# Depthwise taps of one channel block on TensorE in the first two chunks, and stores on other queues

## The chip, the cores and the metric

The kernel runs on one core of a Trainium2 chip. A core has four engines that compute, each with its own list of instructions that it works off in order: TensorE (PE: matrix products into the accumulators, PSUM), VectorE (DVE), ScalarE (ACT) and GpSimd (POOL). A fifth, SyncE (SP), only issues transfers. ACT and POOL issue transfers too. The engines wait for each other by semaphores. The metric is device time in microseconds (us), the median over runs; less is better.

## The reference, cut to what matters

Two layers work on an image batch of 2 x 512 channels x 64 x 64 pixels. The first is a deformable convolution, the second an attention with normalization; the change touches the first alone.

```python
inp = jnp.transpose(x, (0, 2, 3, 1))                 # x is the group-normalized input
xproj = inp @ in_w + in_b
x1 = conv(x, dw_w, 3x3, one filter per channel)      # depthwise
x1 = jnp.transpose(x1, (0, 2, 3, 1)) + dw_b
mu = x1.mean(-1, keepdims=True)
var = ((x1 - mu) ** 2).mean(-1, keepdims=True)
x1 = (x1 - mu) / jnp.sqrt(var + LN_EPS) * ln_g + ln_b
x1 = jax.nn.gelu(x1, approximate=False)
offset = x1 @ off_w + off_b
mask = jax.nn.softmax((x1 @ mask_w + mask_b).reshape(N, H, W, G, P), -1)
out = _dcnv3_core(xproj, offset, mask)               # 9 sampled points per pixel and group
out = out @ out_w + out_b
...
x = x + out
```

The depthwise convolution is nine taps per channel: each output pixel is the sum of nine neighbours, each times a weight of its channel.

## The kernel before, in words

Everything is float32. The 512 channels are four blocks (KB) of 128 partitions; an image is 8 chunks of 512 pixels (8 rows), so the two images are 16 chunks. The first layer is a pipeline over chunks with these stages, each a Python generator whose `yield`s cut it into steps:

- `project(i)` (p0, p1, p2 for the first chunks): ScalarE writes the normalized rows of a chunk with a border row on each side into `xn` (L762, four blocks), then in four tiles TensorE multiplies `xn` with `in_w` into `pq` (L772), ScalarE copies `pq` to `xj` (L778), and two stores write `xj` to the padded image `xt` in memory (L780). There is one `xn`: the next chunk's rows are written over it block by block.
- `features(i)` (f0, f1, f): for each block ScalarE computes the tap in the middle of the upper row with the bias (L798), then VectorE adds the other eight taps, one instruction each (L806). For chunks 0 and 1 (`fill`) TensorE forms the mean over all channels with a matrix of ones (L822, `p_mean`) from the four blocks of `conv`; VectorE subtracts it (L827); ScalarE squares (L832, into `feat`, or `awT` for chunk 1); TensorE forms the mean of the squares (L822 again); ScalarE takes the root (L840, `rstd`), VectorE the reciprocal (L842) and multiplies (L843); ScalarE applies the Gelu (L849, `feat`).
- `weights(i)` (v, w): TensorE multiplies `feat` with the offset and mask weights in four tiles (L866, `po`), VectorE adds the bias (L871); then the exponential (L878), the distances `tx` (L883, L884), a Relu (L890), the softmax sums (L893 to L898), `my` (L901) and 17 instructions that build the window weights `aw` (L909, L914); ScalarE copies them to `at` (L919) and TensorE transposes them (L928).
- `sample(i)` (y, m): TensorE spreads the weights (L957, `pb`), ScalarE or VectorE copies them to `bt` (L962), TensorE multiplies them with patches of `xt` (L976, `pa`; the patches are loaded by `fetch`, L941), then comes the output projection (L996).

Beside them run `image_stats(1)` (`more`: statistics of the second image, VectorE L727, loads from POOL's queue L714), `value_weights` (`products`: a product for the second layer, L1129, with a ScalarE copy `wc_part` L1133 and a store to `wvfc` L1134), and `border()`, 16 stores that write the frame of `xt` (L698, L699).

The pipeline stands in a hand-written order: within `tc.manual_schedule()` the program calls `p0()`, `f0(8)` and so on, and each engine's list is exactly the order in which these calls reach its instructions. The part before the first full `period` is the fill: chunk 0 and 1 have nothing else to run beside. Accumulators with the tag `mm` have four buffers, shared by `pq`, `p_mean`, `pw`, `po` and others in the order of their use. `xj` and `wc_part` share two buffers. `next_to_last` is the order for the last chunk but one: y is the sampling of the chunk before, m that of its own, w the weights of the last chunk.

Of the kernel before, what the change touches and what calls it, by code (L numbers as in the profile page):

```python
# [10 lines left out]
F32 = mybir.dt.float32  # L11
I32 = mybir.dt.int32
AF = mybir.ActivationFunctionType
# [5 lines left out]
P = 128  # L19
NB = 2  # L20
C = 512
KB = C // P
H = W = 64
# [6 lines left out]
NP = 9  # L30
GP = G * NP
CH = 512
NCH = S // CH
ROWS = CH // W
# [484 lines left out]
WIN = W + 4  # L519
# [35 lines left out]
def window_path(  # L555
# [3 lines left out]
    nc = tc.nc  # L559
# [8 lines left out]
    wc_d = dram.tile([P, KB, C], F32, name="wvfc")  # L568
# [13 lines left out]
    ident = const.tile([P, P], F32, name="ident")  # L582
# [43 lines left out]
    with ExitStack() as l0:  # L626
# [68 lines left out]
        def border():  # L695
            for n in range(NB):
                for e in (0, 1, WIN - 2, WIN - 1):
                    nc.sync.dma_start(xt_d[n][e], edge[:WIN, :])  # L698
                    nc.sync.dma_start(xt_d[n][2 : H + 2, e, :], edge[:H, :])  # L699

        gn = {}

# [35 lines left out]
        def project(i):  # L738

            n, ch = divmod(i, NCH)  # L740
            sc, bi = gn[n]
            lo, hi = max(ch * ROWS - 1, 0), min(ch * ROWS + ROWS + 1, H)
            r0 = lo - (ch * ROWS - 1)
            raws = deque()

            def read(kb):
                if i < 3:
                    raws.append(img[kb][:, lo * W : hi * W].rearrange("p (r c) -> p r c", c=W))
                else:
                    t = io.tile([P, ROWS + 2, W], F32, name="raw", bufs=3)  # L750
                    nc.sync.dma_start(t[:, : hi - lo, :].rearrange("p r c -> p (r c)"), x_v[n, :, kb, lo * W : hi * W])
                    raws.append(t[:, : hi - lo, :])

            for kb in range(3):
                read(kb)
            yield
            if ch == 0:
                nc.gpsimd.memset(xn[:, :, 0, :], 0.0)
            if ch == NCH - 1:
                nc.gpsimd.memset(xn[:, :, ROWS + 1, :], 0.0)  # L760
            for kb in range(KB):
                nc.scalar.activation(  # L762
                    xn[:, kb, r0 : r0 + hi - lo, :], raws.popleft(),
                    AF.Identity, bias=bi[:, kb : kb + 1], scale=sc[:, kb : kb + 1],
                )
                if kb + 3 < KB:
                    read(kb + 3)
                yield
            for t in range(ROWS // 2):
                pq = ps.tile([P, C], F32, tag="mm", name="pq")  # L770
                for kb in range(KB):
                    nc.tensor.matmul(  # L772
                        pq, xn[:, kb, 1 + 2 * t : 3 + 2 * t, :].rearrange("p r c -> p (r c)"), in_w[:, kb, :],
                        start=(kb == 0), stop=(kb == KB - 1),
                    )
                yield
                xj = io.tile([P, C], F32, name="xj", bufs=2)
                nc.scalar.copy(xj, pq)  # L778
                for r in range(2):
                    nc.sync.dma_start(xt_d[n][2 + ch * ROWS + 2 * t + r, 2 : W + 2, :], xj[r * W : (r + 1) * W, :])  # L780
                yield

        feats = {}
        conv = cv.tile([P, KB, CH], F32, name="conv")

        def features(i):

            a = cv.tile([P, KB, CH], F32, tag="dT", name="conv1", bufs=2) if i == 1 else conv
            def tap_of(kb, tap):
                dy, dx = tap // 3, tap % 3 - 1  # L790
                acc = a[:, kb, :].rearrange("p (r c) -> p r c", c=W)
                src = xn[:, kb, dy : dy + ROWS, max(dx, 0) : W + min(dx, 0)]
                return acc[:, :, max(-dx, 0) : W + min(-dx, 0)], src, dw_w[:, kb, tap : tap + 1]


            for kb in range(KB):
                dst, src, wt = tap_of(kb, 1)
                nc.scalar.activation(dst, src, AF.Identity, bias=dw_b[:, kb : kb + 1], scale=wt)  # L798
                if i != 2 or kb == KB - 1:
                    yield  # L800
            fill = i < 2
            tot = None if fill else sm.tile([P, CH], F32, tag="tot", name="tot")
            for kb in range(KB):
                for tap in (0, 2, 3, 4, 5, 6, 7, 8):
                    dst, src, wt = tap_of(kb, tap)
                    nc.vector.scalar_tensor_tensor(dst, src, wt, dst, ALU.mult, ALU.add)  # L806
                    if tap < 8:
                        yield

                if not fill:  # L810
                    if kb == 0:
                        nc.gpsimd.dma_start(tot, a[:, 0, :])
                    elif kb < KB - 1:
                        nc.gpsimd.dma_start(tot, a[:, kb, :], accum_op=ALU.add)
                    else:
                        nc.vector.tensor_add(tot, tot, a[:, kb, :])
                yield

            def mean_over_c(tot):
                p = ps.tile([P, CH], F32, tag="mm", name="p_mean")  # L820
                for k, x in enumerate(tot):
                    nc.tensor.matmul(p, ones, x, start=(k == 0), stop=(k + 1 == len(tot)))  # L822
                return p

            mu = mean_over_c([a[:, kb, :] for kb in range(KB)] if fill else [tot])
            yield
            nc.vector.tensor_sub(a, a, mu.unsqueeze(1).to_broadcast([P, KB, CH]))  # L827
            f = awT.rearrange("p g w -> p (g w)").rearrange("p (k c) -> p k c", k=KB)
            if i != 1:
                f = cv.tile([P, KB, CH], F32, tag="feat", name="feat")  # L830
            for kb in range(KB):
                nc.scalar.activation(f[:, kb, :], a[:, kb, :], AF.Square)  # L832
            yield
            if not fill:
                nc.vector.tensor_add(f[:, 0:2, :], f[:, 0:2, :], f[:, 2:4, :])
                nc.vector.tensor_add(f[:, 0, :], f[:, 0, :], f[:, 1, :])
                yield
            var = mean_over_c([f[:, kb, :] for kb in range(KB if fill else 1)])
            rstd = sm.tile([P, CH], F32, tag="tot", name="rstd")
            nc.scalar.activation(rstd, var, AF.Sqrt, bias=eps)  # L840
            yield
            nc.vector.reciprocal(rstd, rstd)  # L842
            nc.vector.tensor_mul(a, a, rstd.unsqueeze(1).to_broadcast([P, KB, CH]))  # L843
            if i == 1:
                f = cv.tile([P, KB, CH], F32, tag="feat", name="feat")
            yield

            for kb in range(KB):
                nc.scalar.activation(  # L849
                    f[:, kb, :].rearrange("p (c q) -> p c q", c=PC), a[:, kb, :].rearrange("p (q c) -> p c q", c=PC),  # L850
                    AF.Gelu, bias=ln_b[:, kb : kb + 1], scale=ln_g[:, kb : kb + 1],
                )
                if kb % 2:
                    feats[i] = f
                    yield
# [231 lines left out]
        def next_to_last(y, v, m, w):  # L1087

            y(3)
            w(8)  # L1090
            v(4)
            for steps, tiles in ((1, 2), (1, 2), (2, 1), (1, 0)):
                m(2)
                w(steps)
                y(tiles)
            for _ in range(4):
                m(2)
                w(2)
            w(5)
# [24 lines left out]
        def value_weights():  # L1124

            for cb in range(KB):
                pw = ps.tile([P, C], F32, tag="mm", name="pw")
                for kb in range(KB):
                    nc.tensor.matmul(  # L1129
                        pw, wv[:, kb, cb * P : (cb + 1) * P], wf[kb], start=(kb == 0), stop=(kb == KB - 1)  # L1130
                    )
                t = io.tile([P, C], F32, tag="xj", name="wc_part", bufs=2)
                nc.scalar.copy(t, pw)  # L1133
                nc.sync.dma_start(wc_d[:, cb, :], t)  # L1134
                yield

        def output_bias():
# [16 lines left out]
        with tc.manual_schedule():  # L1154
# [3 lines left out]
            p0()  # L1158
            for kb in range(KB):
                p0()  # L1160
                f0()
            for t in range(4):
                p0(2)
                f0(8)
            border()
            more()
            p1()
            for kb in range(KB):
                p1()
                f1()  # L1170
                if kb == 1:
                    next(products)
                    next(products)
            f0()
            f1(5)
            p1(4)
            f0()
            f1(11)
            f0()
# [1 line left out]
                more()  # L1181
            p1(4)
            f0(3)
            f1(16)
            next(products)
            fetch(0, 0)
            fetch(0, 1)
# [845 lines left out]
```

## Time and profile before

| what | us |
|---|---|
| median of 3 runs | 3322.8 (3321.55 to 3323.41) |
| the profiled execution | 3318.6 |
| its span in the profile | 3316.8 |
| PE busy | 3148.9 (95%) |
| DVE busy | 2731.0 (82%) |
| ACT busy | 1342.3 (40%) |
| fill: start of the first tap (DVE) to its end of `aw` for chunk 0 | 38.5 to 140.3 |
| first layer, to the last residual addition of the output projection | 1158.3 |

Busy times are from the engine list of the page; the fill's ends are VectorE rows of the timeline. In a timeline a row is a run of like instructions: start in the span, duration, engine, line, operation, output<-input, shape, count, and in brackets the idle time before it with what ended it. An engine's row without a bracket followed the one before directly. In the page's forty slices each digit is the busy share of a slice of some 83 us in tenths, so the fill is the first two slices.

### The profile page before, as it was taken

To read this page: it belongs to the slowest core of one execution; us is meant where nothing else is said; L and a number is where in the kernel's file an instruction comes from. 1 tells how busy PE (TensorE), PEld (TensorE's weight loads), DVE (VectorE), ACT (ScalarE), POOL (GpSimd) and SP (SyncE) were. 2 spreads that over 40 slices of the span, in tenths; PEclk is the share of its full clock that TensorE was granted. 3 is DMA by queue.
4 is the path that set the end of the run, shared out by engine and by line. 5 is a ranking of instruction groups with operands and counts; after the bars stand their busy time and mean duration, and the time that the engine had idled before them with its cause. 6 is when DMAs were issued, how large, how long until landed. Compare 5 with 4: busy or idle time off the path is not lost. (4 is left out here: it accounts for less than half of the span.)

```text
span 3316.8 us, 38421 instructions
## 1 busy us (share of the span) xinstructions
PE 3148.9 (95%) x14207; PEld 2263.5 (68%) x14207; DVE 2731.0 (82%) x3907; ACT 1342.3 (40%) x1848; POOL 291.7 (9%) x420
## 2 busy tenths in 40 slices
PE   5899999999999899999999999999999999999993
PEld 2455555555555676787877877887687787787782
DVE  7999999999998689885976967968897796886874
ACT  2678888888886533203113122123211202203114
POOL 1100000000000000001000011000001101001022
PEclk9999999999999999999999999999999999999996
DMA  7435543443444278658667677557667758648689
GB/s 240 123 117 155 158 117 115 139 147 108 125 136 136 95 284 260 195 171 224 197 174 216 190 218 201 188 195 243 221 202 203 203 180 237 193 163 237 195 311 375
DMA packets 241237, 629.07 MB, mean 190 GB/s; under 512 B 28528, under 2 KB 45552, under 8 KB 240016
## 3 DMA queue, kind: packets, MB, share of 16 engines
q1 hardware_dynamic: 177952, 413.37, 37.5%
q0 software_dynamic: 51936, 179.86, 20.5%
q10 hardware_dynamic: 11152, 33.30, 2.7%
q8 instruction: 114, 1.87, 0.2%
q14 instruction: 83, 0.68, 0.1%
HBM read 406.61 MB, written 124.91 MB: 160 GB/s over the span
## 5 line engine op out<-in xcount | busy, mean ns | idle before, releaser
L1566 PE MATMUL accy<-tt,v 128*128 128x256 f32 x1944 | 580.2, 380 | 0.7 <-DVE ct L1632 0.6
L1456 ACT ACTIVATE e<-pS 128x1024 f32<-128x1024 f32 x256 | 248.3, 1021 | 736.1 <-PE pS L1451 731.9
L1566 PE MATMUL accx<-e,v 128*128 128x256 f32 x1728 | 453.5, 385 | 0.5 <-DMA v<-wv 0.5
L1566 PE MATMUL accy<-e,v 128*128 128x256 f32 x1728 | 445.2, 380 | 0.0
L1566 PEld LDWEIGHTS accy<-tt,v 128*128 128x128 f32 x1944 | 369.6, 190 | 53.8 <-DVE tt L1524 2.2
L1566 PEld LDWEIGHTS accx<-e,v 128*128 128x128 f32 x1728 | 320.5, 190 | 118.3 <-issue 77.9
L806 DVE SCALAR_TENSOR_TENSOR conv<-xn,L_conv_dw_w_sb,conv 128x504 f32<-128x504 f32 (+1 forms) x512 | 376.8, 744 | 29.2 <-ACT conv L798 15.3
L1566 PEld LDWEIGHTS accy<-e,v 128*128 128x128 f32 x1728 | 329.5, 191 | 45.2
L1524 DVE TENSOR_TENSOR tt<-tt,e 128x512 f32<-128x512 f32 x432 | 298.9, 692 | 14.8
L1566 PE MATMUL accx<-tt,v 128*128 128x256 f32 x972 | 290.7, 381 | 14.0 <-DVE tt L1523 14.0
L1523 DVE TENSOR_TENSOR tt<-e 128x256 f32<-128x256 f32 x432 | 181.0, 419 | 141.1 <-PE accy L1566 138.8
L976 PEld LDWEIGHTS pa<-bt,patch 96*128 96x128 f32 x2048 | 248.4, 195 | 57.1 <-issue 38.8
L976 PE MATMUL pa<-bt,patch 96*128 96x128 f32 x2048 | 252.4, 280 | 7.6 <-issue 4.0
L1451 PE MATMUL pS<-q,keys 64*128 64x512 f32 x1024 | 254.7, 615 | 0.3 <-DVE stats L1789 0.3
L962 ACT COPY bt<-pb 96x1024 f32<-96x1024 f32 x120 | 226.2, 2024 | 45.8 <-PE pb L957 45.8
L772 PE MATMUL pq<-in_w,xn 128*128 128x512 f32 x512 | 234.6, 601 | 3.4 <-ACT xn L762 3.4
L996 PE MATMUL py<-dT,L_conv_out_w_sb 128*128 128x512 f32 x512 | 230.0, 593 | 0.0
L1571 ACT COPY u<-accx 128x256 f32<-128x256 f32 x54 | 20.1, 372 | 477.0 <-PE accx L1566 474.2
L1566 PEld LDWEIGHTS accx<-tt,v 128*128 128x128 f32 x972 | 184.6, 190 | 41.0 <-DVE tt L1523 16.0
L987 ACT COPY dT<-pa 32x256 f32<-32x256 f32 x496 | 179.5, 362 | 62.3 <-PE pa L976 53.4
L866 PE MATMUL po<-om_w_pg,feat 128*128 128x432 f32 x512 | 203.6, 542 | 0.8 <-ACT feat L849 0.8
L996 PEld LDWEIGHTS py<-dT,L_conv_out_w_sb 128*128 128x128 f32 x512 | 95.5, 190 | 114.3 <-issue 107.4
(292 smaller groups left out, 4381.5 us busy)
## 6 DMA issues: line engine op xcount, KB each, us to landing
v<-wv SPq DMA_DIRECT2D x420, 448.0 KB
tot<-e POOLq DMA_DIRECT2D x160, 512.0 KB, 6.8
patch<-xt SPq DMA_DIRECT2D x256, 192.0 KB
wv<-vform SPq DMA_DIRECT2D x48, 512.0 KB
v<-ww SPq DMA_DIRECT2D x54, 448.0 KB
wv<-vsum SPq DMA_DIRECT2D x48, 384.0 KB
xt<-xj SPq DMA_DIRECT2D x128, 128.0 KB
res<-in_x SPq DMA_DIRECT2D x64, 256.0 KB
```

The lines of the kernel that those rows point to most:

```text
L772: nc.tensor.matmul(pq, xn[:, kb, 1 + 2 * t : 3 + 2 * t, :].rearrange("p r c -> p (r c)"), in_w[:, kb, :], start=(kb == 0), stop=(kb == KB ...
L806: nc.vector.scalar_tensor_tensor(dst, src, wt, dst, ALU.mult, ALU.add)
L866: nc.tensor.matmul(po[:, : 3 * GP], f[:, kb, t * P : (t + 1) * P], om_w[:, kb].rearrange("p a k g -> p (a k g)"), start=(kb == 0), stop=(k ...
L962: copy(bt[:SN].rearrange("s g q d -> s d (g q)")[:, d0 : d0 + 4, :], pb[:SN])
L976: nc.tensor.matmul(pa[:, p], xp[:SN, p, cb * P : (cb + 1) * P], bt[:SN, 4 * cb : 4 * cb + 4, PX * s + p, :], start=True, stop=True,)
L987: copy(dst, src)
L996: nc.tensor.matmul(py, out_w[:, kb, cb * P : (cb + 1) * P], dT[:, kb, :], start=(kb == 0), stop=(kb == KB - 1))
L1451: nc.tensor.matmul(p[:, a, :], keys[r, i, (2 * u + h) * P : (2 * u + h + 1) * P], c.q[r, qh, :], start=True, stop=True,)
L1456: nc.scalar.activation(e.rearrange("p a q -> p (a q)"), p.rearrange("p a q -> p (a q)"), AF.Exp)
L1523: nc.vector.tensor_sub(t[:, 0], x[:, 1], x[:, 3])
L1524: nc.vector.tensor_add(t[:, 1:3], t[:, 0].unsqueeze(1).to_broadcast([P, 2, HQ]), x[:, 0:3:2])
L1566: nc.tensor.matmul(out, v[:, blk, :], op, start=(first and g == 0), stop=(final and g == NG))
```

## The change

In chunks 0 and 1 the ninefold sum of channel block 3 is formed by TensorE: for each tap it multiplies the shifted rows of `xn` with a diagonal matrix that has the tap's weights on its diagonal, all nine into one accumulator, and ScalarE copies the sum out with the bias. `diagonals()` builds the nine matrices on ScalarE from the identity. Blocks 0 to 2, and all four blocks of the later chunks, are formed as before. The hand-written order calls `deep(0)` after the second projection tile of chunk 0 and `deep(1)` after the second of chunk 1, ahead of the second step of f0 in that place (L827 and L832).

Stores move: the 16 border stores from SP to POOL, the projection stores of chunk 2 and the four `wvfc` stores from SP to ScalarE's queue. In `next_to_last` two steps of w (the exponential and `tx`) move from the loop to ahead of it, and the loop's third round has none.

```diff
         def border():
...
-                    nc.sync.dma_start(xt_d[n][e], edge[:WIN, :])
-                    nc.sync.dma_start(xt_d[n][2 : H + 2, e, :], edge[:H, :])
+                    nc.gpsimd.dma_start(xt_d[n][e], edge[:WIN, :])
+                    nc.gpsimd.dma_start(xt_d[n][2 : H + 2, e, :], edge[:H, :])
...
                 for r in range(2):
-                    nc.sync.dma_start(xt_d[n][2 + ch * ROWS + 2 * t + r, 2 : W + 2, :], xj[r * W : (r + 1) * W, :])
+                    queue = nc.scalar if i == 2 else nc.sync
+                    queue.dma_start(xt_d[n][2 + ch * ROWS + 2 * t + r, 2 : W + 2, :], xj[r * W : (r + 1) * W, :])
...
+        def diagonals():
+            t = sm.tile([P, NP, P], F32, tag="tx", name="diag")
+            for tap in range(NP):
+                nc.scalar.activation(t[:, tap], ident, AF.Identity, scale=dw_w[:, KB - 1, tap : tap + 1])
+            diagonal.append(t)
+
+        def deep(i):
+            kb = KB - 1
+            p = ps.tile([P, CH], F32, tag="mm", name="p_dw")
+            to = p.rearrange("p (r c) -> p r c", c=W)
+            for k, tap in enumerate((1, 0, 2, 3, 4, 5, 6, 7, 8)):
+                dy, dx = tap // 3, tap % 3 - 1
+                nc.tensor.matmul(
+                    to[:, :, max(-dx, 0) : W + min(-dx, 0)], diagonal[0][:, tap],
+                    xn[:, kb, dy : dy + ROWS, max(dx, 0) : W + min(dx, 0)], start=(k == 0), stop=(k == NP - 1),
+                )
+            nc.scalar.activation(convs[i][:, kb, :], p, AF.Identity, bias=dw_b[:, kb : kb + 1])
...
+            direct = range(KB - 1) if i < 2 else range(KB)
...
-            for kb in range(KB):
+            for kb in direct:
                 dst, src, wt = tap_of(kb, 1)
                 nc.scalar.activation(dst, src, AF.Identity, bias=dw_b[:, kb : kb + 1], scale=wt)
...
-            for kb in range(KB):
+            for kb in direct:
                 for tap in (0, 2, 3, 4, 5, 6, 7, 8):
...
             v(4)
-            for steps, tiles in ((1, 2), (1, 2), (2, 1), (1, 0)):
+            w(2)
+            for steps, tiles in ((1, 2), (1, 2), (0, 1), (1, 0)):
                 m(2)
                 w(steps)
                 y(tiles)
...
                 nc.scalar.copy(t, pw)
-                nc.sync.dma_start(wc_d[:, cb, :], t)
+                nc.scalar.dma_start(wc_d[:, cb, :], t)
...
             for kb in range(KB):
                 p0()
-                f0()
-            for t in range(4):
+                if kb < KB - 1:
+                    f0()
+            diagonals()
+            for k in range(4):
                 p0(2)
-                f0(8)
+                if k == 1:
+                    deep(0)
+                if k < 3:
+                    f0(8)
             border()
             more()
             p1()
             for kb in range(KB):
                 p1()
-                f1()
+                if kb < KB - 1:
+                    f1()
                 if kb == 1:
                     next(products)
                     next(products)
             f0()
             f1(5)
             p1(4)
+            deep(1)
             f0()
             f1(11)
             f0()
...
             p1(4)
             f0(3)
-            f1(16)
+            f1(8)
             next(products)
```

More of the change, by code (lines that the diff above doesn't have):

```diff
@@ L784, in window_path @@
         conv = cv.tile([P, KB, CH], F32, name="conv")
+        convs, diagonal = {}, []
+        def diagonals():
[14 more added lines that the diff above has]
+            nc.scalar.activation(convs[i][:, kb, :], p, AF.Identity, bias=dw_b[:, kb : kb + 1])
         def features(i):
             a = cv.tile([P, KB, CH], F32, tag="dT", name="conv1", bufs=2) if i == 1 else conv
+            convs[i] = a
+            direct = range(KB - 1) if i < 2 else range(KB)
             def tap_of(kb, tap):
```

## The prediction

> **What bounds the kernel now.** I read the page's engine rows first, then the timeline of VectorE, TensorE and ScalarE over the first 420 us (the change acts there), then the same three over 1040 to 1215 us, where `next_to_last` runs. Times are starts within the span, durations beside them.
>
> The engine rows of the page say that TensorE is the long engine of the whole program, VectorE the long one of the first tenth:
>
> ```profile
> span 3316.8 us, 38421 instructions
> PE   5899999999999899999999999999999999999993
> DVE  7999999999998689885976967968897796886874
> ```
>
> VectorE's fill is a row of taps with hardly a hole:
>
> ```profile
> 43.41 23.68 DVE L806 SCALAR_TENSOR_TENSOR conv<-xn,L_conv_dw_w_sb,conv 128x512 f32<-128x512 f32 x31
> 67.01 2.28 DVE L827 TENSOR_TENSOR conv<-conv,p_mean 128x2048 f32<-128x2048 f32 x1
> 69.20 8.43 DVE L806 SCALAR_TENSOR_TENSOR conv<-xn,L_conv_dw_w_sb,conv 128x504 f32<-128x504 f32 x11
> ...
> 84.17 3.33 DVE L842 RECIPROCAL rstd<-rstd 128x512 f32<-128x512 f32 x1
> ...
> 89.75 12.33 DVE L806 SCALAR_TENSOR_TENSOR conv<-xn,L_conv_dw_w_sb,conv 128x504 f32<-128x504 f32 x16
> ...
> 106.56 0.61 DVE L871 TENSOR_TENSOR o<-po,om_b_pg 128x432 f32<-128x432 f32 x1 [1.12 <-PE po L866]
> ```
>
> 31 taps in 23.68 us are 0.764 us each. The subtraction of the mean (L827) comes at 67.01 with no wait before it, so the mean was there in time.
>
> TensorE in the same stretch has work queued in a fixed order, and its one hole is at 71.65:
>
> ```profile
> 37.63 16.85 PE L772 MATMUL pq<-in_w,xn 128*128 128x512 f32 x32 [2.29 <-ACT xn L762]
> 54.33 7.03 PE L1129 MATMUL pw<-wf,wv 128*128 128x512 f32 x16
> 61.19 3.60 PE L822 MATMUL p_mean<-conv,ones_c 128*128 128x512 f32 x8
> 64.62 7.03 PE L772 MATMUL pq<-in_w,xn 128*128 128x512 f32 x16
> 76.31 5.99 PE L822 MATMUL p_mean<-feat,ones_c 128*128 128x512 f32 x8 [4.65 <-ACT feat L832]
> 82.14 7.03 PE L772 MATMUL pq<-in_w,xn 128*128 128x512 f32 x16
> ...
> 113.62 13.90 PE L772 MATMUL pq<-in_w,xn 128*128 128x512 f32 x32
> ```
>
> A 512-column matmul shows as two records; 13.90/32 = 0.434 us a record, 0.87 a matmul. The first mean ended at 64.79, 2.2 us ahead of VectorE's need. ScalarE is the third link: it carries results from TensorE to the next TensorE or VectorE step, in order.
>
> ```profile
> 54.57 0.58 ACT L778 COPY xj<-pq 128x512 f32<-128x512 f32 x1 [2.85 <-PE pq L772]
> 56.06 0.81 ACT L798 ACTIVATE conv<-xn,L_conv_dw_b_sb,L_conv_dw_w_sb 128x512 f32<-128x512 f32 x1
> ...
> 74.49 1.23 ACT L778 COPY xj<-pq 128x512 f32<-128x512 f32 x2 [9.19 <-DMA wvfc<-wc_part]
> 75.62 2.19 ACT L832 ACTIVATE feat<-conv 128x512 f32<-128x512 f32 x4
> ```
>
> The first line is the last projection copy of chunk 0, the second the first upper-middle tap of chunk 1 (L798), which VectorE's taps of chunk 1 need. At 74.49 ScalarE had waited 9.19 us for a store that stood on SP's queue behind the 16 border stores (issued from 56.37 to 70.02); the squares at 75.62 were late by that.
>
> **Removed from VectorE.** Eight taps of block 3 in each of two chunks: 16 x 0.764 = 12.2 us. If VectorE alone set the pace, the fill would end that much earlier.
>
> **Added to TensorE and ScalarE.** `deep(i)`: 9 matmuls, 18 records x 0.434 = 7.8 us, twice. Bounds: the longest rate in the fill is the second mean's 5.99/8 = 0.75 a record (13.5 us); the lowest per column is this same pq row. The operand has the width of pq's, so I take 7.8. Diagonals: nine 128x128 activations, a shape the trace does not have. The 128x256 copy u takes 0.37 us, the 128x512 activation 0.81, so they take 3.3 to 7.3 us; I take 0.43 each (nearer the smaller), 42.4 to 46.2. Their cover is TensorE's first two projection tiles, done at 47.6; even at 0.81 each they end at 49.7, before the last matmuls of `deep(0)` want theirs. Cost 0; without that cover up to 2.1.
>
> **Where the added work stands.** In the changed program each engine's list is fixed, and the new work is ahead of what VectorE waits for.
>
> First `deep(0)` stands between projection tiles 2 and 3. The copy of the last tile, 54.57, becomes 62.4, and behind it on ScalarE stand xn and that tap of chunk 1: 56.06 becomes 63.9, ready at 64.7. VectorE, with 24 taps in place of 32, is done at about 57.5 and idles 7 us. The first mean ends at 64.79 + 7.8 = 72.6, and the subtraction moves from 67.01 to 72.7: 5.6 late.
>
> Then TensorE runs two projection tiles (7.0, to 79.5) and `deep(1)` (to 87.2). ScalarE's list has the copy out of `deep(1)` ahead of the four squares of chunk 0: copy 87.3 to 88.0 (0.69, the 128x512 rstd row that also reads PSUM), squares 2.19 to 90.2. The second mean follows the squares: 88.7 + 3.5 = 92.2, where it ended at 76.31 + 5.99 = 82.3 before. **That is 9.9 us late.** VectorE cannot hide it: subtraction to 74.9, 11 taps to 83.3, six statistics with their load wait as before (77.55 to 84.17, 6.6 us) to 89.9, then a wait for rstd, 92.2 + 0.7, to 93.0. The reciprocal moves from 84.17 to 93.0.
>
> Behind the second mean TensorE has two projection tiles, whose copies stand ahead of the Gelu on ScalarE; Gelu feeds po, po feeds L871. All of this is the same as before, so 106.56 becomes 116.5. VectorE's eight remaining taps of chunk 1 end at about 104.7 and hide there. From 116.5 on the list on every engine is the old one, run without holes of its own that could take a late start back: +9.9 at the start of period 0, and to the end of the sampling.
>
> Two rows bound the second mean: its own 5.99 us, with the granted clock at 0.70 between 75 and 85 us, and the first mean's 3.60. At the old 5.99 the shift is 12.4; if its last matmul follows the last square directly (90.2 + 0.9), it is 8.9. I take the first mean's, since TensorE has no hole ahead of it any more. [...]
>
> **Moved stores.** The 16 borders go past SP to POOL: 16 x 0.54 us (POOL's issue row early L714) from 43.5 to about 52.5. On POOL behind them now stand the first three statistics loads, issued at 2.67 before; they land some 3.6 us after issue, at 58, and are wanted at 83.3: covered by 25 us. SP loses 13.7 us of issues; projection stores and, at 114, the patch loads stand behind them, none late. The four wvfc stores and the eight projection stores of chunk 2 go to ScalarE: 12 x 0.57 (wq, 1.14 for 2). This lies in ScalarE's holes: four of its issues are by the statistics and the Gelu wait, the other eight between 131 and 145, where before it waited 4.38 and 2.37 us for the same stores' landing. It removes the 9.19 us wait too, but the squares now wait for `deep(1)` anyway. Net 0.
>
> Against the borders on POOL speaks this: in the fill POOL's issues beside taps took 0.54 to 0.90 us and landed after 3.2 to 3.6. [...]
>
> **The end of the sampling.** `next_to_last` moves the exponential and the tx step of the last chunk ahead of its loop.
>
> ```profile
> 1068.16 1.92 DVE L962 COPY bt<-pb 96x1024 f32<-96x1024 f32 x1 [3.18 <-PE pb L957]
> ...
> 1074.63 1.41 DVE L883 TENSOR_SCALAR tx<-o 128x1152 f32<-128x1152 f32 x2
> 1076.07 1.36 DVE L884 SCALAR_TENSOR_TENSOR tx<-tx 128x1152 f32<-128x1152 f32 x1
> ...
> 1084.42 1.85 DVE L962 COPY bt<-pb 96x1024 f32<-96x1024 f32 x1
> 1086.37 17.04 PE L976 MATMUL pa<-bt,patch 96*128 96x128 f32 x128 [4.02 <-issue]
> ```
>
> VectorE idled 3.18 us before 1068.16, and 17.04 us of matmuls start as soon as the fourth copy (1084.42, ends 1086.27) is out. tx's 2.72 us go into the hole; they wait for the transposes that read the same buffer (end 1066.2), so the first copy is 0.8 late, the second, which waits for TensorE at 1072.86, is not. Then 2.7 us are gone from VectorE's list, but the last pb before the fourth copy ended at 1082.35 and waits for the third's buffer, so 1.9 to 2.7 come back; I take 2.1. The exponential goes into ScalarE's hole.
>
> **Sum.** +9.9 - 2.1 = +7.8. The profiled execution took 3318.6 us (span 3316.8 and 1.8 around it): 3326.4. The median of the runs is 4.2 above it: 3330.6, rounded to **3330.5**. The attention behind starts later by the same amount and is unchanged.
>
> **Rivals.**
> A, the forecast, at 0.58: 3322.8 + 8.9 - 2.7 = 3329.0 to 3322.8 + 12.4 - 1.9 = 3333.3.
> B, `deep(1)` is hidden, only the first delay counts: reciprocal at 89.9, +5.7, less 2.1 is 3326.4. For it speaks VectorE's own length up to 89.9; against it that ScalarE's list puts the copy of `deep(1)` ahead of the squares. 0.17.
> C, VectorE keeps the pace and TensorE's added work disappears in its hole of 4.65 us and the waits of ScalarE: -12.2 - 2.1, 3308.5. For it: VectorE was 9.6 of 10 us busy from 45 to 75, and the squares lose their 9.19 us wait. Against: from 37.6 to 71.6 TensorE has no hole, and the mean had a reserve of 2.2 where 7.8 come in. It decides if chunk 1's first tap starts at 58 and not near 64. 0.12.
> D, more comes on top: the stores on ScalarE wait there for transfers on other queues and hold Gelu and the at copies, or POOL starves. Twelve issues unhidden are 6.8 us: 3337. ScalarE's holes speak against it. 0.13.
>
> 0.2% of 3322.8 is 6.6 us, about what a measurement of this kernel tells from no change; the bound is 3329.4. Of A I put 0.47 above and 0.11 below; with D 0.60 slower, with B 0.28 the same, C 0.12. The range leaves out C and the far part of D: 3321 to 3336.
>
> **What would show it.** VectorE idle for about 7 us near 58 and again before the subtraction at 72.7; that subtraction's reciprocal near 93; the second mean on TensorE near 88.7, at full clock; L871's third at 116.5; the 17 us of pa 7.8 later than before. If the reciprocal is near 84 or before, the forecast is wrong and C right; if ScalarE idles on DMA between 128 and 150, D.

## The result, and the profile after

| | median us | runs | lowest to highest |
|---|---|---|---|
| before | 3323.4 | 11 | 3319.8 to 3325.2 |
| changed | 3328.5 | 11 | 3324.6 to 3334.0 |

The forecast was 3330.5 us, with a range of 3321 to 3336. The ratio is 1.0017, 95% interval 1.0009 to 1.0025: 3 to 8 us slower. The profiled execution took 3334.0 us (span 3332.2), the highest of the eleven, while that of before lay below all eleven runs of before made beside it, so the 15.4 us between the two profiles are not the difference of the kernels. In what follows, marks are therefore counted from each profile's own first tap (38.51 before, 37.23 after), and every kernel below has its own profile.

Lines of code behind the new functions stand 26 lower in the changed kernel: L806 is L832, L827 L853, L842 L868, L871 L897, L976 L1002; those behind `next_to_last` 27 lower. The page's engine rows, in the same forty slices as before:

```profile
span 3332.2 us, 38489 instructions
...
PE   5899999999999899999999999999999999999992
...
DVE  6799999999998688886876977868897796886874
```

TensorE's row is what it was but for the last slice; VectorE's first slice goes from 7 to 6 and its second from 9 to 7. Next VectorE's timeline in the fill (start, duration, engine, line, operation, shape, count, idle time before it and what ended it):

```profile
42.13 13.77 DVE L832 SCALAR_TENSOR_TENSOR conv<-xn,L_conv_dw_w_sb,conv 128x512 f32<-128x512 f32 x18
63.32 3.87 DVE L832 SCALAR_TENSOR_TENSOR conv<-xn,L_conv_dw_w_sb,conv 128x504 f32<-128x504 f32 x5 [7.42 <-ACT conv L824]
71.25 2.29 DVE L853 TENSOR_TENSOR conv<-conv,p_mean 128x2048 f32<-128x2048 f32 x1 [4.05 <-PE p_mean L848]
...
91.47 3.35 DVE L868 RECIPROCAL rstd<-rstd 128x512 f32<-128x512 f32 x1 [3.10 <-ACT rstd L866]
...
97.07 6.21 DVE L832 SCALAR_TENSOR_TENSOR conv<-xn,L_conv_dw_w_sb,conv 128x504 f32<-128x504 f32 x8
...
114.90 0.61 DVE L897 TENSOR_TENSOR o<-po,om_b_pg 128x432 f32<-128x432 f32 x1 [3.40 <-PE po L892]
```

VectorE has fewer taps and spends the time in waits: 7.42 us for chunk 1's first tap, 4.05 for the first mean, 3.10 for the root, 3.40 for `po`. TensorE in the same stretch:

```profile
46.23 7.81 PE L803 MATMUL p_dw<-xn,diag 128*128 128x512 f32 x18
53.88 7.03 PE L772 MATMUL pq<-in_w,xn 128*128 128x512 f32 x16
60.75 7.03 PE L1156 MATMUL pw<-wf,wv 128*128 128x512 f32 x16
67.61 3.60 PE L848 MATMUL p_mean<-conv,ones_c 128*128 128x512 f32 x8
71.05 7.03 PE L772 MATMUL pq<-in_w,xn 128*128 128x512 f32 x16
77.91 7.81 PE L803 MATMUL p_dw<-xn,diag 128*128 128x512 f32 x18
87.02 3.70 PE L848 MATMUL p_mean<-feat,ones_c 128*128 128x512 f32 x8 [1.29 <-ACT feat L858]
```

Each `p_dw` takes 7.81 us, and the row behind it starts later by that much. The second mean takes 3.70 us where it took 5.99; the granted clock was 1.00 in 85 to 110 us, and 0.70 in 75 to 85 us before. ScalarE, around chunk 1's first tap and then around the chunk 2 stores:

```profile
41.07 2.72 ACT L793 ACTIVATE diag<-ident,L_conv_dw_w_sb 128x128 f32<-128x128 f32 x9
...
60.99 0.59 ACT L778 COPY xj<-pq 128x512 f32<-128x512 f32 x1 [2.85 <-PE pq L772]
...
62.48 0.81 ACT L824 ACTIVATE conv<-xn,L_conv_dw_b_sb,L_conv_dw_w_sb 128x512 f32<-128x512 f32 x1
...
85.76 0.69 ACT L807 ACTIVATE conv<-p_dw,L_conv_dw_b_sb 128x512 f32<-128x512 f32 x1 [7.06 <-PE p_dw L803]
86.34 2.18 ACT L858 ACTIVATE feat<-conv 128x512 f32<-128x512 f32 x4
...
132.94 2.39 ACTq L781 DMA_DIRECT2D xt<-xj  x2
135.43 0.59 ACT L778 COPY xj<-pq 128x512 f32<-128x512 f32 x1 [3.83 <-DMA patch<-xt]
138.33 2.56 ACTq L781 DMA_DIRECT2D xt<-xj  x2
140.93 1.28 ACT L875 ACT_TABLE_LOAD   x1 [4.92 <-DMA xt<-xj]
...
151.77 2.99 ACT L945 COPY at<-aw 128x400 f32<-128x400 f32 x4 [0.45 <-DVE conv L832]
```

The copy out of `deep(1)` (L807) stands directly ahead of the squares (L858). Behind 131 ScalarE idles 3.83 and 4.92 us around four stores, its Gelu comes late, and the at copies (L945) start at 151.77, although VectorE was done with `aw` at 148.66 (a sum: start and length of its last row). Before, the same copies followed `aw` at once (140.56). At the end of the sampling:

```profile
1085.67 1.43 DVE L909 TENSOR_SCALAR tx<-o 128x1152 f32<-128x1152 f32 x2 [1.31 <-PE p_tr L954]
1087.14 1.36 DVE L910 SCALAR_TENSOR_TENSOR tx<-tx 128x1152 f32<-128x1152 f32 x1
1088.41 1.92 DVE L988 COPY bt<-pb 96x1024 f32<-96x1024 f32 x1
...
1103.38 16.53 PE L1002 MATMUL pa<-bt,patch 96*128 96x128 f32 x128 [2.01 <-issue]
```

The two tx rows now stand ahead of the copies, and the long `pa` group starts 17.0 us later than in the profile of before, where the output projection ahead of it was 19.4 later: 2.4 us won.

### The profile page after: what moved, and what is told of

The parts are those of the page before. It is cut to its first block, busy times and chain, and to the rows that moved or that the text cites. A ratio compares the mean times of both kernels' runs of the same rounds, so it can differ in the third digit from the quotient of the medians.

```text
span 3332.2 us, 38489 instructions
## 1 busy us (share of the span) xinstructions
PE 3169.4 (95%) x14243; PEld 2273.1 (68%) x14243; DVE 2720.3 (82%) x3891; ACT 1345.1 (40%) x1857; POOL 300.9 (9%) x436
## 4 chain that ended last, share of the span: by engine, by line
PE 80%; DVE 10%; ACT 4%; DMA 3%; issue 2%; POOL 0%; POOLq 0%; ACTq 0%; SPq 0%; DVEq 0%
PE accy L1600 22%; PE accx L1600 17%; PE pa L1002 7%; PE pS L1485 7%; PE py L1022 7%; PE pq L772 6%; PE po L892 4%; PE pvy L1834 3%; PE pvx L1834 2%; PE pb L983 2%; PE pk L1915 2%; ACT bt L988 1%; DVE conv L832 1%; PE p_mean L848 1%; DMA xr<-wx 1%
## 5 line engine op out<-in xcount | busy, mean ns | idle before, releaser
L832 DVE SCALAR_TENSOR_TENSOR conv<-xn,L_conv_dw_w_sb,conv 128x504 f32<-128x504 f32 x496 | 365.1, 744 | 37.4 <-ACT conv L824 24.0
L1002 PEld LDWEIGHTS pa<-bt,patch 96*128 96x128 f32 x2048 | 247.9, 195 | 56.0 <-issue 37.5
L1002 PE MATMUL pa<-bt,patch 96*128 96x128 f32 x2048 | 251.9, 279 | 6.5 <-ACT bt L988 2.4
L892 PE MATMUL po<-om_w_pg,feat 128*128 128x432 f32 x512 | 211.7, 559 | 0.8 <-ACT feat L875 0.7
```

Of the source, the lines that this page charges most:

```text
L892: nc.tensor.matmul(po[:, : 3 * GP], f[:, kb, t * P : (t + 1) * P], om_w[:, kb].rearrange("p a k g -> p (a k g)"), start=(kb == 0), stop=(k ...
L1002: nc.tensor.matmul(pa[:, p], xp[:SN, p, cb * P : (cb + 1) * P], bt[:SN, 4 * cb : 4 * cb + 4, PX * s + p, :], start=True, stop=True,)
```

## The experiments

The table gives the times of the changed kernel and of twelve others, each beside runs of before on the same chip, and how many us later (+) than in the profile of before five marks start, counted from the first tap. Before, they stand at 28.5, 45.7, 68.1, 102.0 and 125.7. The third add of po is VectorE's third bias row (L871 before, L897 after). The times are medians of several runs; the marks come from one profiled execution of each kernel.

| run | median | before | ratio (95%) | first mean's subtraction | reciprocal | third add of po | at copies | first pa |
|---|---|---|---|---|---|---|---|---|
| changed | 3328.5 | 3323.4 | 1.0017 (1.0009 to 1.0025) | +5.5 | +8.6 | +9.6 | +12.5 | +14.6 |
| e1 | 3328.2 | 3321.6 | 1.0020 (1.0011 to 1.0029) | +4.9 | +8.0 | +9.3 | +9.7 | +9.5 |
| e2 | 3322.1 | 3321.6 | 1.0001 (0.9993 to 1.0010) | 0.0 | +0.2 | +1.7 | +4.5 | +4.5 |
| e3 | 3320.3 | 3321.6 | 0.9996 (0.9987 to 1.0004) | 0.0 | +1.6 | +2.1 | +2.0 | +3.8 |
| e4 | 3324.1 | 3321.6 | 1.0009 (1.0001 to 1.0018) | +4.9 | +8.0 | +9.0 | +8.9 | +8.7 |
| e5 | 3323.6 | 3321.7 | 1.0008 (0.9998 to 1.0017) | +4.9 | +4.7 | +6.1 | +8.6 | +10.1 |
| e6 | 3320.2 | 3321.7 | 0.9997 (0.9987 to 1.0007) | 0.0 | +0.6 | +1.6 | +4.3 | +4.2 |
| e7 | 3322.4 | 3321.7 | 1.0002 (0.9993 to 1.0011) | -0.5 | -8.7 | -3.0 | +3.1 | +3.7 |
| e8 | 3316.0 | 3321.7 | 0.9980 (0.9971 to 0.9989) | +0.1 | -8.1 | -5.1 | -2.8 | +0.9 |
| e9 | 3331.4 | 3322.6 | 1.0023 (1.0014 to 1.0033) | +5.7 | +8.7 | +9.7 | +12.0 | +11.7 |
| e10 | 3313.7 | 3322.6 | 0.9971 (0.9959 to 0.9984) | +0.6 | -7.6 | -4.6 | -4.8 | -3.9 |
| e11 | 3320.2 | 3322.6 | 0.9994 (0.9984 to 1.0003) | +0.2 | -8.0 | -2.6 | -1.0 | +1.2 |
| e12 | 3326.1 | 3321.6 | 1.0009 (1.0000 to 1.0019) | +4.9 | +8.0 | +9.0 | +8.9 | +8.7 |

The marks up to the third add repeat within 0.8 us between kernels with the same list (changed, e1, e4, e9, e12). What e3 shows, +2.1 and +3.8 with a fill that is line for line that of before, is how far executions of one list can differ.

**e1: the TensorE taps alone.**

Against the changed kernel:

```diff
-                    nc.gpsimd.dma_start(xt_d[n][e], edge[:WIN, :])
-                    nc.gpsimd.dma_start(xt_d[n][2 : H + 2, e, :], edge[:H, :])
+                    nc.sync.dma_start(xt_d[n][e], edge[:WIN, :])
+                    nc.sync.dma_start(xt_d[n][2 : H + 2, e, :], edge[:H, :])
...
-                    queue = nc.scalar if i == 2 else nc.sync
+                    queue = nc.sync
...
-            w(2)
-            for steps, tiles in ((1, 2), (1, 2), (0, 1), (1, 0)):
+            for steps, tiles in ((1, 2), (1, 2), (2, 1), (1, 0)):
...
-                nc.scalar.dma_start(wc_d[:, cb, :], t)
+                nc.sync.dma_start(wc_d[:, cb, :], t)
```

> The kernel before with the TensorE taps alone (diagonals, deep(0) and deep(1) where the change has them); borders, projection stores and wvfc stores stay on SP, the end of the sampling stays as before. Chain theory (the added matmuls stand ahead of the first mean and of the squares): the third add of po's bias comes 9 to 10 us later after the first tap than the 68.05 us of before, and the time is 3323.4 + 9 = about 3332. Rival 'the stores cost it' (the added matmuls are hidden, the 5 us come from the stores on ScalarE's queue): the third add within 2 us of before and the time within 3 us of before. Rival 'VectorE's pace': 12 us faster.

Third add +9.3, time +6.7 us. The added matmuls by themselves cost the whole delay of the fill, and the other two theories fall. The time was expected 9 us above before; e3 shows where the missing 2 us may lie (see the sum further down).

**e2: the moved stores and the moved step alone.**

Against the changed kernel; f0 and f1 have their old counts of steps again:

```diff
-            direct = range(KB - 1) if i < 2 else range(KB)
+            direct = range(KB)
...
-            diagonals()
...
-                if k == 1:
-                    deep(0)
...
-            deep(1)
```

> The changed kernel with all four blocks of taps on VectorE again (no diagonals, no deep); the moved stores and the moved step at the end of the sampling stay. Chain theory: the third add of po's bias 0 to 1 us off the 68.05 us of before (the 9.19 us wait goes, but VectorE sets the pace there), then up to 4 us lost between 115 and 165 to the stores on ScalarE, then -2.9 at the end of the sampling: 3320 to 3325. Rival 'the stores cost it': about 8 us at the first pa, 3328. If the 9.19 us wait had been on the path: 4 to 9 us faster than before at the reciprocal.

The reciprocal comes 0.2 us off that of before: the 9.19 us wait on the stores is gone (the squares start as the subtraction lets them) and nothing came of it. The row behind them that waits longest, the table load ahead of the Gelu, waits for VectorE, not for TensorE:

```profile
71.04 2.19 ACT L858 ACTIVATE feat<-conv 128x512 f32<-128x512 f32 x4
...
88.97 1.28 ACT L875 ACT_TABLE_LOAD   x1 [6.01 <-DVE conv L869]
```

From the third add to the at copies 2.8 us are lost, as in the changed kernel (2.9). So that loss belongs to the moved stores and not to `deep`. The third add itself is 1.7 us late where 0 to 1 was expected; the part on the clock below says why.

**e3: the moved step alone.**

Against the kernel before:

```diff
+            w(2)
-            for steps, tiles in ((1, 2), (1, 2), (2, 1), (1, 0)):
+            for steps, tiles in ((1, 2), (1, 2), (0, 1), (1, 0)):
```

> The kernel before with the moved step at the end of the sampling alone (the exponential and tx of the last chunk ahead of the loop). Every theory: nothing before 1040 us, then the last pa group 1.9 to 2.9 us earlier: 3320.5 to 3321.5, ratio 0.9991 to 0.9994. If the gain is given back behind the sampling: ratio 1.000.

The interval holds the expectation and also no change. In the trace the shift falls from +4.4 ahead of the loop to +2.5 behind it: 1.9 us, and it stays (+2.3 at the end of the attention).

**e4: chunk 2's projection stores back on SP.**

```diff
-                    queue = nc.scalar if i == 2 else nc.sync
+                    queue = nc.sync
```

> The changed kernel with the eight projection stores of chunk 2 on SP's queue again (the four wvfc stores stay on ScalarE, the borders on POOL). If those stores on ScalarE held it (copies waiting 3.83 and Gelu 4.92 us between 131 and 142): the shift at the first pa falls from 14.6 us (counted from the first tap) to about 10 and the time falls by 4 against the changed kernel, to 3324.5. If the wait is the transfers' own (the 16 patch loads keep the engines of the DMA busy, and on SP the stores stand behind them, as before): the shift at the first pa stays within 1 us of the changed kernel's and so does the time.

The shift at the at copies is +8.9, that of the third add +9.0: the 3 us are gone, with a change of nothing else. At the first pa it is 5.9 us less than in the changed kernel's profile, of which some 2 are explained below by the clock.

**e5 and e6: one block each.**

```diff
-            direct = range(KB - 1) if i < 2 else range(KB)
+            direct = range(KB - 1) if i == 0 else range(KB)
...
-            deep(1)
```

This is e5. In e6 it is `i == 1`, and `deep(0)` is not called; the other chunk's steps have their old counts.

> The changed kernel with deep(0) alone: chunk 1's block 3 is on VectorE again. Chain theory: the first subtraction 5.5 us late as in the changed kernel, the reciprocal some 4.8 late (statistics' wait for a load takes the rest), third add +4.7 from there on (all counted from the first tap), time about +2 to +5 with the stores on ScalarE and the moved last step. If the whole shift came from deep(1): third add within 1 us of before. If both blocks cost alike: third add +4.8 as well, but then deep(1) alone gives +4.8 too.

> The changed kernel with deep(1) alone: chunk 0's block 3 is on VectorE again. Chain theory: first subtraction on time; second mean starts behind deep(1), the copy and the squares: reciprocal 0.5 to 2 us late, since VectorE is behind there by itself and TensorE has its 4.65 us hole; third add +1.5. The two blocks alone then sum to 6.2, less than the 9.6 of both together: the second costs in full only when the first has already used the reserve. If each costs what it costs in the changed kernel (5.5 and 4.1): third add +4.1.

Reciprocal +4.7 and +0.6, third add +6.1 and +1.6. The reciprocals sum to 5.3 where both together give 8.6: `deep(1)` alone hides in the hole that TensorE had ahead of the second mean, and costs 3.9 us (8.6 less 4.7) once `deep(0)` has made VectorE wait already. That e5's third add is 1.4 us later than its reciprocal would have it is the clock again (below).

**e7: both blocks, placed later.** Against the changed kernel, the fill from the second half of chunk 0's tiles on:

```diff
             for k in range(4):
                 p0(2)
-                if k == 1:
-                    deep(0)
...
-            for kb in range(KB):
+            for kb in range(KB - 1):
                 p1()
...
+            deep(0)
+            p1()
             f0()
-            f1(5)
-            p1(4)
-            deep(1)
+            f1(12)
+            p1(2)
             f0()
-            f1(11)
+            f1(9)
             f0()
...
+            p1(6)
+            f0(3)
+            deep(1)
```

So `deep(0)` comes behind all four tiles of chunk 0 and three xn writes of chunk 1, the second mean ahead of three tiles of chunk 1, `deep(1)` behind those and Gelu. The six statistics, ahead of the reciprocal until now, follow behind it in two threes. Of the value products three stand behind chunk 2's tiles and one behind the at copies; chunk 2's stores are on SP.

> Both blocks stay on TensorE, but placed where nothing waits for them: deep(0) behind the fourth projection tile and three of chunk 1's xn writes, deep(1) behind all projection tiles of chunk 1 and Gelu; the four value products (pw) go behind them, to the end of the fill; the second mean stands ahead of three of chunk 1's tiles; chunk 2's stores are on SP. Placement theory (the change lost by its place in TensorE's list, and TensorE has only some 14 us of holes between 37 and 147 for 15.6 us more): first pa within 1.5 us of before, counted from the first tap, time 2 us faster by the moved last step: 3318 to 3321. If VectorE's 12.2 us were all that counts: first pa 8 to 12 us earlier. If TensorE's 15.6 us are paid wherever they stand: first pa 8 us later.

The reciprocal is 8.7 us earlier than before; 6.6 of this is that the six statistics and their wait (77.55 to 84.17 before) now stand behind it. The third add is 3.0 earlier: the same work in another order turns +9.6 into -3.0. Then it is lost again. TensorE's timeline:

```profile
121.95 7.03 PE L1156 MATMUL pw<-wf,wv 128*128 128x512 f32 x16
131.70 5.40 PE L1156 MATMUL pw<-wf,wv 128*128 128x512 f32 x8 [2.72 <-ACT xj L778]
136.94 3.63 PE L1168 MATMUL p_bias<-L_conv_in_b_sb,L_conv_out_w_sb 128*128 128x1 f32 x32
140.43 3.68 PE L1156 MATMUL pw<-wf,wv 128*128 128x512 f32 x8
143.94 1.91 PE L954 MATMUL p_tr<-ident,at 128*128 128x128 f32 x16
```

The value products that made room for the taps stand here in a row, the third waits 2.72 us, and the transposes (L954; L928 at 141.50 before) start at 143.94, 4.8 us later counted from the first tap. The time is that of before. VectorE's pace alone (8 to 12 us earlier) is refuted. The placement theory was too hopeful as well: it had the first pa within 1.5 us of before and 3318 to 3321 us, measured are +3.7 and 3322.4. The 14 us of holes in the expectation are those of TensorE's timeline before, up to the first `pb`: 4.65, 7.09, 0.66, 0.67 and three of 0.25.

**e8: one block, placed later.** Against e7; of the value products one stands ahead of po, two behind chunk 2's tiles and one behind the at copies.

```diff
-            direct = range(KB - 1) if i < 2 else range(KB)
+            direct = range(KB - 1) if i == 0 else range(KB)
...
-            deep(1)
```

> As the kernel with both blocks later, but only deep(0) is on TensorE, chunk 1's block 3 is on VectorE; the value products one ahead of po, two between chunk 2's tiles, one behind the at copies. Placement theory: 7.8 us more fit TensorE's holes (some 14 us), VectorE is 6.1 us shorter: reciprocal 8 to 9 us earlier, third add 5 to 6 earlier, first pa 5 to 6 earlier, with the moved last step 7 to 8 us faster than before: 3314 to 3316, ratio 0.9976. If TensorE's list is the limit whatever the order: no earlier than before.

0.9980: faster than both kernels, by 5.6 us against before. Reciprocal and third add are as expected, the first pa is not (+0.9). On ScalarE a copy of chunk 2 and one of a product waited 3.77 and 3.61 us for stores of chunk 2 to land, and TensorE's p_bias waited 2.16 us for the first of them.

**e9: patch loads called behind the stores.**

```diff
-            fetch(0, 0)
-            fetch(0, 1)
             p2()
...
             p2(4)
+            fetch(0, 0)
+            fetch(0, 1)
```

> The changed kernel with one move: the sixteen patch loads of chunk 0 are issued behind chunk 2's projection stores instead of ahead of them. Theory 'waits for other queues' loads' (a store on ScalarE can't be issued until an earlier transfer, here a patch load on SP, has landed): the waits of 3.83 and 4.92 us on ScalarE between 131 and 142 vanish, the at copies follow VectorE's aw directly (shift 9.6 in place of 12.6 us, from the first tap). Theory 'a DMA issue on ScalarE is slow by itself' (1.1 to 1.3 us each): they stay. In both the patch loads land later, 125 to 145, ahead of the first pa.

Inconclusive: the loads are on SP and the stores on ScalarE, so the call order doesn't bind them; SP issued the loads from 121.75 on, ahead of the first store at 131.71, as in the changed kernel. The waits stayed (3.21 and 4.91).

**e10 and e11: half of the patch loads behind the stores, on one queue.** e8 and e7 with

```diff
             fetch(0, 0)
-            fetch(0, 1)
...
             p2(4)
+            fetch(0, 1)
```

> The kernel with one block on TensorE, placed later, and eight of chunk 0's sixteen patch loads issued behind chunk 2's stores. There VectorE's aw ended 5.1 us earlier than in before but the first pa started 0.9 later: copies of ScalarE waited 3.77 and 3.61 us for stores that stood behind the patch loads, and TensorE stood still behind them. If that is the cause: first pa 3 to 5 us earlier than before (from the first tap), time 3311 to 3314, ratio 0.997. If TensorE's list itself is too long: first pa within 1 us of before, ratio 0.998 as there.

> The kernel with both blocks on TensorE, placed later, with the same split of the patch loads. If the 6.3 us lost there between VectorE's aw and the at copies came from the stores behind the loads alone: first pa 3 us earlier than before. If TensorE's list is the limit (15.6 us more against some 14 us of holes): the transposes start when pw and p_bias are through, first pa 0 to 2 us later than before.

Here both are on SP, and the order binds: in e10 SP issued eight loads from 107.51 on, the stores from 116.74 and the other eight loads from 129.99. e10: at copies -4.8 and first pa -3.9, time 0.9971 (0.9959 to 0.9984), 5 to 14 us faster than before and the fastest version. Its TensorE list:

```profile
120.81 7.03 PE L1156 MATMUL pw<-wf,wv 128*128 128x512 f32 x16
127.68 3.63 PE L1168 MATMUL p_bias<-L_conv_in_b_sb,L_conv_out_w_sb 128*128 128x1 f32 x32
131.17 5.38 PE L1156 MATMUL pw<-wf,wv 128*128 128x512 f32 x8
136.38 1.91 PE L954 MATMUL p_tr<-ident,at 128*128 128x128 f32 x16
```

Not all of the 4.8 us between e8 and e10 at the first pa belong to the stores. p_bias starts 1.8 us earlier than in e8, by the wait that is gone. From there to the transposes e10 takes 8.7 us and e8 12.1: the granted clock was at half for 10.2 us from 130.2 in e8, for 3.4 us from 131.9 in e10. Whether the wait brought on the longer stretch is not shown. The two times (0.9980 and 0.9971) have overlapping intervals.

e11: at copies -1.0, first pa +1.2. Its transposes start at 141.75, right behind the last product without a wait, so there TensorE's list sets the end: in this order two blocks are one too many.

e7, e8, e10 and e11 change much at once, and no run has their order with all taps on VectorE. What VectorE's rows add up to, from its first tap to the end of `aw` for chunk 0, helps: before 95.7 us of work and 6.1 of waits, the changed kernel 84.0 and 27.5, e8 89.5 and 7.2, e10 89.5 and 7.7. So in e8 and e10 `aw` is 5 us earlier because the list is 6.2 us shorter, not because the new order removed waits.

**e12: the same stores on POOL.**

```diff
-                    queue = nc.scalar if i == 2 else nc.sync
+                    queue = nc.gpsimd if i == 2 else nc.sync
```

> The changed kernel with the eight projection stores of chunk 2 on POOL's queue. Theory 'shared counters' (transfers issued by SP and by ScalarE take eight completion counters in turn, and an issue waits for the transfer that had the counter before, a patch load issued some 7.5 us earlier; POOL's transfers have counters of their own): the stores issue without that wait, the copies xj follow each other, Gelu of chunk 1 starts when VectorE hands over, the at copies follow aw: shift 9.6 in place of 12.6 us from the first tap, first pa +9 to +11, time 3 us below the changed kernel. Rival 'the memory transfers themselves are slow beside the patch loads': xj copies still wait 3 us and more for stores to land before Gelu; shift 11 to 12.6.

ScalarE's timeline:

```profile
130.59 1.05 ACT L778 COPY xj<-pq 128x512 f32<-128x512 f32 x2
135.03 5.00 ACT L875 ACTIVATE feat<-conv,L_conv_ln_b_sb,L_conv_ln_g_sb 128x512 f32<-128x512 f32 x4 [2.09 <-DVE conv L869]
...
148.32 3.01 ACT L945 COPY at<-aw 128x400 f32<-128x400 f32 x4 [0.82 <-DVE L_conv_out_b_sb L1172]
```

Two copies in a row, then Gelu when VectorE hands over; shift +8.9 at the at copies, as on SP (e4). The time, 3326.1, is 2.4 us below the changed kernel's. The trace names the semaphores. In that of the changed kernel each of the four stores ahead of the Gelu waits on ScalarE for a semaphore that a patch load on SP, issued 7.6 to 8.5 us earlier, was the last to use, and is issued within 0.1 us of that load's landing (stores at 132.94, 134.88, 138.33 and 140.44, landings at 132.87, 134.85, 138.26 and 140.42): there the transfers of SP and ScalarE report to the same eight semaphores in turn (107, 109, 111 to 116), POOL's to others (99 to 106). SP's issues took longer beside those stores too: its sixteen patch loads took 17.41 us to issue in the changed kernel, 12.93 here.

## Why the prediction was right

**The fill** was sized at 9.9 and measured 9.6. Step by step (forecast times first, then the changed profile moved to before's first tap, +1.28): chunk 1's first tap 64.7 and 64.60; subtraction 72.7 and 72.53; second mean 88.7 and 88.30; reciprocal 93.0 and 92.75; third add 116.5 and 116.18. 7.8 us for `deep` was 7.81. The nine diagonals took 2.72 us in place of 3.9 and hid, as said. e1 shows that nothing else makes this shift, e5 and e6 that the two parts stack as the forecast had them, e7 that it hangs on the order and not on the amount of work: the chain through TensorE and ScalarE was right.

**The clock.** The second mean took 3.70 us behind a wait of 1.29, where before it took 5.99 behind 4.65; the granted clock was 1.00 there, and before it was at half for 6.8 us from 74.2. Two other kernels show the same at the first po group: in e2 and e5 TensorE waited 6.00 and 3.41 us ahead of it, the granted clock was at half for 6.8 us from 90.9 and 94.4, and 16 records took 9.03 and 8.98 us where they take 5.96 at a granted clock of 1.00 (before, from 103.46); that is why the third add slips by another 1.4 to 1.5 us in these two. That the clock would stay whole without the hole of 4.65 us was the author's estimate, and with it the 9.9 in place of 12.4; no run changes the wait alone, so it is not shown that the wait brings the slow stretch on. What the runs showed is 3.70 us at 1.00 in the changed kernel, 3.70 as well behind waits of 1.21 and 1.29 in e2 and e6, and 6.42 behind 6.70 in e3.

**The moved stores** were put at net 0, and that term was mis-sized. From the third add to the at copies it measured +2.9 us (+2.8 in e2, -0.1 in e4 and e12). The step that failed is "This lies in ScalarE's holes": the issues do, but not the wait of each issue for a transfer on SP's queue. Rival D named this, with 128 to 150 us as its place, and priced it by twelve issues at 6.8 us; it is four waiting issues and about 3. So a part of D came true beside A. The borders on POOL cost nothing (e4, which keeps them there, has the fill's marks of e1 within 0.3 us):

```profile
42.52 0.59 POOL L698 DMA_DIRECT2D xt<-raw  x1 [8.04 <-DVE raw L693]
43.10 0.56 POOL L699 DMA_DIRECT2D xt<-raw  x1
...
52.31 0.54 POOL L699 DMA_DIRECT2D xt<-raw  x1 [0.91 <-DMA xt<-raw]
```

The sixteen issues took 0.54 to 0.59 us each beside VectorE's taps: the forecast's 0.54 held, not the 0.90 that was set against it.

**The end of the sampling**, -2.1: -2.4 in the changed profile, -1.9 in e3.

**The sum.** 9.6 + 2.9 - 2.4 is 10.1, the forecast had 7.8, and the medians differ by 5.1, or 3.0 to 8.3 by the interval. The forecast was made against a profile that was itself 4.2 us below the median of the runs shown. e3's profile shows how that may come: with before's fill it stands at +3.8 at the first pa, after ScalarE waited 11.13 us (9.19 in the profile of before) for the same store and the statistics' load came later. The changed kernel has no such wait there. So against a usual execution of before its fill loses less than 9.6. An estimate from these two profiles: with e3 in place of before, the first pa is 14.6 - 3.8 = 10.8 us later, and 8.4 remain behind the end of the sampling, at the upper end of the interval. How the rest divides between such differences of executions and the clock below was not measured by itself and stays open. So the mechanism of the fill was right, and that the total came within 2 us is in part luck: two errors of opposite sign, one of them the stores. The chances fit less well: 0.60 stood for slower by more than 0.2% and 0.28 for the same, and the ratio of 1.0017 lies in the second, with an interval that reaches into the first.

B had the reciprocal 5.7 us late; it is 8.6 (8.0 in e1), and e5 and e6 show that `deep(1)` is hidden only without `deep(0)`. C falls by the waits of 7.42 and 4.05 us on VectorE.

## What to carry to other kernels

Work moved to an engine with slack is not free there: where it stands ahead of what another engine waits for, it costs its length less the reserve that it meets (7.8 less 2.2 for `deep(0)`, measured 4.9 to 5.5; little for `deep(1)` alone, which met a hole). Count the engine's holes first (here some 14 us between 37 and 147, against 15.6 added), then place the work behind the last thing that someone waits for: one block of taps made the third add 6.1 us later in one order (e5) and 5.1 and 4.6 us earlier in another (e8, e10, where other work moved too). Count the waits of a store moved to a computing engine's queue as well: here four stores on ScalarE's queue waited for patch loads on SP's queue, by a shared semaphore, ScalarE idled 3.83 and 4.92 us around them, and the work behind them came 2.9 us later.

## What had not been expected

In the changed profile the shift grows by 1.7 us at five places between 230 and 1070, in periods that are the same in both kernels. At each the granted clock is at half for 3.4 us. Stretches of the windows view (time, PE, PEld, DVE, ACT and POOL busy, PEclk, DMA share, GB/s), first of the changed kernel, then the same place of before:

```profile
424.00:434.00 10.00, 9.52 (x45) 4.45 (x44) 9.40 (x17) 6.64 (x5) 0.87 (x1) 0.83 0.42 128
557.00:567.00 10.00, 9.53 (x45) 4.57 (x44) 9.47 (x14) 6.59 (x5) 0.85 (x1) 0.83 0.45 140
```

```profile
412.00:422.00 10.00, 9.54 (x50) 4.77 (x49) 9.61 (x18) 8.38 (x5) 1.41 (x2) 1.00 0.53 168
```

The eight po records there take 4.86 us in place of 3.17. TensorE was not idle ahead of it: in the 3.4 us before 427.9 it ran `pb`, whose matmuls use 25 rows, and the first of these po records, with a pause of 0.48. The five stretches start at 427.9, 561.1, 759.0, 892.2 and 1025.3, some 133, 198, 133 and 133 us apart, by the clock record 39 or 58 times the 3.41 us that one lasts. The same periods had none of them in the profile of before and in e10, one each in e3, e4 and e8, two in e1 and e5, three in e12, four in e2, e6 and e9, five in e7 and e11. What brings a stretch on is not shown. At 1.7 us each, zero to five of them would by estimate be up to 8.5 us between executions, about the spread that the changed kernel shows (3324.6 to 3334.0). The mean granted clock of each of its eleven executions agrees: the two fastest have 0.985, the four slowest 0.982, and 0.003 of 3330 us is 10 us of TensorE at full clock. Where in those executions the clock was lost is known only for the profiled one. The stretch at 144.6 in the changed profile lasted 17.1 us in place of 10.2 and covers the first `pb` and `po`: that is where most of the 2.1 us between its at copies (+12.5) and its first pa (+14.6) is likely to go.
